# Gated linear attention with a routed mixture of experts on one core: where an exponential, a sigmoid and the first rows of a slot table stand in their queues, and which PSUM banks take transposed x

## The chip, the cores and the metric

The kernel runs on one core of a Trainium2 chip, in float32 apart from the half-precision tables described below. Its time is the device time of one execution in microseconds (us); several executions are timed and their median is given. A profile is one further execution, recorded by the hardware profiler, with every instruction's start and duration. Engines are called PE (TensorE, matrix products), DVE (VectorE), ACT (ScalarE), POOL (GpSimd) and SP (SyncE, which issues most DMA transfers). Each engine runs its own instructions strictly in the order of its queue, and waits on semaphores for the others.

## The reference

The input x has 8 sequences of 512 tokens with 512 features. With `xn = layernorm(x)` the output is `x + s * silu(f)`:

- `s` is linear attention with decay on xn: q, k, v and a gate are products of xn with weights; q and k pass a SiLU and a rotation; 16 heads of 32 features work in chunks of 128 tokens with a running state; the result is multiplied by a sigmoid gate, normalised by head, and projected by Wo.
- `f` is a mixture of 16 experts (each a SwiGLU with 128 hidden features), of which each token uses its 4 best, weighted by a softmax over those 4, plus one shared expert weighted by a sigmoid.

```
logits = xn @ gate_w.T                      # 16 per token
top 4 of softmax(logits), renormalised      # = exp(l - max) / sum over the 4
f = sum_r w_r * expert_{e_r}(xn) + sigmoid(xn @ shared_gate) * shared(xn)
out = x + attention(xn) * silu(f)
```

## The kernel before

**Stages.** (1) `first` walks the 8 sequences in pieces: it normalises x (`norm`), transposes it on PE (`turn`), computes router logits and the 4 best experts (`route_1` to `route_3`), and the shared expert (`share_1`, `share_2`). Sequence 0's attention (`enter`, `sequence(0)`) is interleaved with those pieces. (2) `sort` turns the choices of all 4096 tokens into places in lists by expert, in blocks of 128 rows. (3) `table` inverts the places into a slot table: which token stands in which row of which block. It runs beside the attention of sequence 1. (4) The 136 and more blocks are gathered, passed through their experts, scaled and written. (5) The attention of sequences 2 to 7 runs while the expert rows are gathered back and added up.

**What sets the order.** The program is traced line by line; a planner then fixes the order of each engine's queue by when it thinks each instruction is ready, the earlier traced one first among those that are. Two helpers overrule it. `on_pe()` (L206) queues a PE instruction behind the PE instruction traced last under it, so the order of nearly all PE work is that of the source. `behind(engine)` (L214) queues what its block traces behind the instruction of that engine traced last before it. Neither adds a wait for a result; they fix who stands ahead of whom. Anything else floats.

**PSUM banks.** `bank(tag, name)` (L106) gives a bank of 128 x 512 floats: four with the tag a, one k, one m, two d. A bank is handed on when its last reader is done. In `turn` (L272) each of a sequence's four tiles takes a bank, PE writes four 128 x 128 transposes into it, and ACT copies it out (L286). Other users of these tags near it: `share_1` writes pg to m and pu to d (L345, L346), `share_2` writes its four tiles to d, a, m, a (L364), `key` products go to m and `query` products and `output` to d, `value` to m and d by turns, the four score products of a head group to all four a (L704).

**Sort's tail.** `sort` is a generator. Its steps are drawn one at a time by `also()` inside `sequence(0)`; what is left after its loop over r (L419 to L433) is traced by L1041, after `sequence(0)` has ended, so after the four projections of sequence 0 and their copies out (`spill`, L983, an ACT copy to `so`). That tail is: the exponential of the 4 logits per token (L435, ACT), the sum, reciprocal and product (L437 to L439, DVE), the sigmoid of the shared gate (L441, ACT) and its store (L442), seven POOL instructions that spread the weights over the 16 experts into `wt` (L446, L450), the store of `wt` beside the rows of xn in DRAM (L451), and the store of the places `posi` (L454).

**Change of rooms.** All tiles of stages 1 and 2 live in the pool `p1`. L1043 closes it, and the pool `exps` is opened in its place with one tile, `wexp`, for the weights of all 16 experts (L1047). It covers the room in which posi, oh, w4, sgs, wt, wr and the others stood. Its first users are the weight loads of eleven experts (L1050, on SP's queue), and in the room of the last experts the tables of `table`: two small casts on ACT (L496, L498) and an iota on POOL that writes the counts 0, 1, 2, ... (L499). Seven stores of zeros to `y_d` follow on SP (L1054), and behind them the load of transposed x of sequence 2 (L584).

**The slot table.** 128 lists of 32 tokens' places (`sp`) are treated 16 at a time by `make(i)`: for each half of the 16, a comparison of the counts with the place inside half a block (L516), for the first half a product with the token number (L519), and a comparison with the number of the half block (L522), all on DVE. `number` multiplies the other half by its token numbers on ACT (L530, eight small instructions). PE then adds 16 products up in `pn` (L553), and DVE adds that to `acc` (L562, L564). `table` is a generator too: after its set-up, one step is drawn after each quarter of a key, query or value product of `sequence(1)` by `between[0]()` (L605, L649). So the first call of `make` (i = 0) is traced in the key product of group 2, behind the scores of group 0; the second (i = 16) in the query product of group 2. The first `pn` products stand under `on_pe()` between the third and fourth quarters of that query product. The last result gives `slot` (L573), by which the block rows are gathered.

**The PE order around it** is: projections of sequence 0 (pw, L800), states and scores of sequence 1's group 0 (L699, L710), key product of group 2 (L646), transposes of group 1's keys (L678, which reuse the bank of the states that DVE reads in L723 and L725), three quarters of the query product of group 2, the first pn (L553), and on.

Of the kernel before, what the change touches and what calls it, by code (L numbers as in the profile page):

```python
# [15 lines left out]
AF = mybir.ActivationFunctionType  # L16
ALU = mybir.AluOpType
# [28 lines left out]
HALF = P // 2  # L46
GROUP = 16
# [49 lines left out]
def tile_block(ctx: ExitStack, tc: tile.TileContext, a: dict, out: bass.AP):  # L97
    nc = tc.nc
# [7 lines left out]
    def bank(tag, name):  # L106
        return pp.tile([P, 512], F32, tag=tag, name=name, bufs={"a": 4, "k": 1, "m": 1, "d": 2}[tag])
# [39 lines left out]
    def load_x(b):  # L147
        t = p1.tile([P, NC, D], F32, tag="x", name=f"x_{b}", bufs=3)
        rows = x[b].rearrange("(t p) d -> p t d", p=P)
        for ts in [slice(i, i + 1) for i in range(NC)] if b == 0 else [slice(0, NC)]:  # L150
            nc.sync.dma_start(t[:, ts, :], rows[:, ts, :])
        xs_of[b] = t
# [36 lines left out]
    w4 = p1.tile([P, NT, TOPK], F32, tag="w4", name="w4")  # L189
    sgs = p1.tile([P, NT], F32, tag="sgs", name="sgs")  # L190
    posi = p1.tile([P, TOPK, NT], I32, tag="posi", name="posi")

    sp = const.tile([P, 2, TOPK * NT], F16, tag="slot", name="sp")
# [11 lines left out]
    @contextmanager  # L205
    def on_pe():  # L206

        with tc.issue_after(last_pe[-1]) if last_pe else nullcontext():
            yield
        traced = nc.cur_bb.bb.instructions  # L210
        last_pe.append(next(
            i for i in reversed(traced) if i.engine == mybir.EngineType.PE))

    def behind(engine):  # L214

        last = next(
            (i for i in reversed(nc.cur_bb.bb.instructions) if i.engine == engine), None)
        return tc.issue_after(last) if last else nullcontext()

    POOL, DVE, ACT = (  # L220
        mybir.EngineType.Pool, mybir.EngineType.DVE, mybir.EngineType.Activation)
# [50 lines left out]
    def turn(b):  # L272

        xs = xs_of[b]
        if b:
            xT = p1.tile([P, KC, N], F32, tag="xT1", name=f"xT1_{b}", bufs=2)
        else:
            xT = xT_of[b] = att.tile([P, KC, N], F32, tag="xT", name=f"xT_{b}", bufs=1)
        xT1_of[b] = xT
        for t in range(NC):  # L280
            ps = bank("a", f"psT_{b}_{t}")
            with on_pe():
                for k in range(KC):
                    nc.tensor.transpose(
                        ps[:, k * P : (k + 1) * P], xs[:, t, k * P : (k + 1) * P], ident)
            nc.scalar.copy(  # L286
                xT[:, :, t * P : (t + 1) * P], ps.rearrange("p (k n) -> p k n", n=P))
        if b:
            xs_of.pop(b)
            if b + 3 < B:  # L290
                load_x(b + 3)
            nc.sync.dma_start(xT_d[b], xT.rearrange("p k n -> p (k n)"))
# [80 lines left out]
    def sort():  # L373
# [5 lines left out]
        for to, by, name in ((total, ones, "total"), (af, tri, "before")):  # L379
            ps = bank("a", f"p{name}")  # L380
# [38 lines left out]
        for r in range(TOPK):  # L419
# [12 lines left out]
                    sp.rearrange("p w (r t) -> p w r t", t=NT)[:, :, r], bl[:, :, r])  # L432
            yield  # L433

        nc.scalar.activation(w4, w4, AF.Exp)  # L435
        den = p1.tile([P, NT], F32, tag="den", name="den")
        nc.vector.tensor_reduce(den, w4, axis=AX.X, op=ALU.add)  # L437
        nc.vector.reciprocal(den, den)
        nc.vector.tensor_tensor(  # L439
            w4, w4, den.unsqueeze(2).to_broadcast([P, NT, TOPK]), ALU.mult)  # L440
        nc.scalar.activation(sgs, sgs, AF.Sigmoid)  # L441
        nc.sync.dma_start(sg_d, sgs)  # L442
        wt = p1.tile([P, NT, E], F32, tag="h1", name="wt", bufs=2)
        wr = p1.tile([P, NT, E], F32, tag="sl", name="wr", bufs=2)
# [25 lines left out]
    def table(room):  # L470

        half = room.bitcast(F16)
        free = [0]
        quads = GROUP // QUAD


        def part(*shape):
            n = int(np.prod(shape))  # L480
            free[0] += n
            flat = half[:, free[0] - n : free[0]]
            return flat.rearrange("p (q j) -> p q j", j=QUAD) if len(shape) == 2 else (
                flat.rearrange("p (u q j) -> p u q j", u=quads, j=QUAD))

        homes = [(part(quads, HALF, QUAD), part(quads, 2 * NB, QUAD))]
        count = part(2 * NB, QUAD)
        free[0] = 2 * WE * (LATE - LATE // 2)
        homes.append((part(quads, HALF, QUAD), part(quads, 2 * NB, QUAD)))

        def flat(n):
            free[0] += n
            return half[:, free[0] - n : free[0]]

        half_token, fold, acc = flat(NT), flat(HALF), flat(2 * NB)
        nc.scalar.copy(half_token, token)  # L496
        for h in range(0, P, HALF):
            nc.scalar.copy(fold[h : h + HALF], ident[h : h + HALF, h : h + HALF])  # L498
        nc.gpsimd.iota(  # L499
            count, [[1, 2 * NB], [0, QUAD]], base=0, channel_multiplier=0,  # L500
            allow_small_or_imprecise_dtypes=True)

        def rows(of, n):
            return of.rearrange("p (u j) -> p u j", j=QUAD).unsqueeze(2).to_broadcast(
                [P, of.shape[-1] // QUAD, n, QUAD])

        def make(i):
            place, block = homes[i // GROUP % 2]
            for u in range(0, quads, quads // 2):
                us = slice(u, u + quads // 2)  # L510
                lists = slice(i + u * QUAD, i + (u + quads // 2) * QUAD)

                def counts(n):
                    return count[:, :n].unsqueeze(1).to_broadcast([P, quads // 2, n, QUAD])

                nc.vector.tensor_tensor(  # L516
                    place[:, us], counts(HALF), rows(sp[:, 0, lists], HALF), ALU.is_equal)
                if u == 0:
                    nc.vector.tensor_tensor(  # L519
                        place[:, us], place[:, us], rows(half_token[:, lists.start % NT :][  # L520
                            :, : GROUP // 2], HALF), ALU.mult)
                nc.vector.tensor_tensor(  # L522
                    block[:, us], counts(2 * NB), rows(sp[:, 1, lists], 2 * NB), ALU.is_equal)

        def number(i, some):
            place = homes[i // GROUP % 2][0]
            for j in range(max(some[0], GROUP // 2), some[1]):
                row = place[:, j // QUAD, :, j % QUAD]
                t = (i + j) % NT
                nc.scalar.activation(row, row, AF.Copy, scale=token[:, t : t + 1])  # L530

        yield
        make(0)
        for j in range(0, GROUP, 4):
            number(0, (j, j + 4))
            yield
        for i in range(0, TOPK * NT, GROUP):
            more = i + GROUP < TOPK * NT
            if more:
                make(i + GROUP)  # L540
            else:
                for e in range(E - LATE, E - LATE // 2):
                    nc.sync.dma_start(wexp[:, e, :], a["experts"][:, e, :])
            if i < TOPK * NT // 2:
                yield
            place, block = homes[i // GROUP % 2]
            pn = bank("a", f"pn_{i}")
            for some in ((0, 5), (5, 10), (10, GROUP)):
                if some[0] == 5:
                    with on_pe():  # L550
                        for j in range(GROUP):
                            h = j % 2 * HALF
                            nc.tensor.matmul(  # L553
                                pn[h : h + HALF, : 2 * NB],
                                lhsT=place[:, j // QUAD, :, j % QUAD],
                                rhs=block[:, j // QUAD, :, j % QUAD], start=(j < 2),
                                stop=(j >= GROUP - 2))
                if more:
                    number(i + GROUP, some)
                if some[1] == GROUP:  # L560
                    if i:
                        nc.vector.tensor_tensor(acc, acc, pn[:, : 2 * NB], ALU.add)  # L562
                    else:
                        nc.vector.tensor_copy(acc, pn[:, : 2 * NB])  # L564
                yield
        pt = bank("a", "pslot")
        with on_pe():
            for h in range(2):
                nc.tensor.matmul(
                    pt[h * HALF : (h + 1) * HALF, :NB], lhsT=fold,  # L570
                    rhs=acc.rearrange("p (b h) -> p b h", h=2)[:, :, h], start=True, stop=True)
        t = const.tile([P, NB], I32, tag="slot", name="slot")
        nc.vector.tensor_scalar(t, pt[:, :NB], float(B * N // 2), None, ALU.add)  # L573
        slots.append(t)
# [411 lines left out]
    def first():  # L986
# [22 lines left out]
        next(sorting)  # L1009

    sorting = sort()
    norm(0)
    turn(0)
    norm(1)
    halves(0)
# [196 lines left out]
    place = comb.tile([P, TOPK, NT], I32, tag="place", name="place")  # L1212
# [166 lines left out]
```

## Time and profile before

| what | us |
|---|---|
| median of 3 timed executions (1164.88 to 1168.21) | 1166.71 |
| the profiled execution's own time | 1162.74 |
| its span, from the first to the last instruction | 1160.9 |
| PE busy | 1128.0 |
| DVE busy | 710.2 |
| ACT busy | 456.3 |
| POOL busy | 454.1 |
| idle time of PE ahead of the transposes of the last sequence (at 155.9) | 1.05 |
| idle time of PE ahead of a value product (at 185.8) | 1.04 |
| idle time of PE ahead of the key transposes of sequence 1, group 1 (at 237.7) | 4.54 |
| idle time of PE ahead of a value product of sequence 2 (at 266.3) | 1.85 |
| first pn products start | 243.67 |
| first gather of block rows starts | 301.95 |

Times such as "at 243.67" count from the start of the span. In the answers of the trace a line of the timeline gives the start, the time taken, the engine, the line of the kernel, the operation, output and input, their shape and how many were merged, and in brackets how long the engine had stood idle and what ended that. A line with the name of an engine and a q (SPq) is that engine's queue issuing a transfer.

### The profile page before, as it was taken

What the parts mean: (1) busy time and instruction counts of PE and PEld (TensorE: products, weight loads), DVE (VectorE), ACT (ScalarE), POOL (GpSimd) and SP (SyncE); (2) the same over time, 40 slices, a digit from 0 to 9 for tenths busy, and PEclk for the clock granted to TensorE, in tenths of its full rate; (3) what the DMA queues carried; (4) which work ended last, traced back from release to release, by engine and by line L of the source; (5) the groups of instructions that cost most, each with busy time, mean ns of one, the idle gap of its engine ahead of it and who ended that gap; (6) DMA issues with size and microseconds to landing.
All of it is one profiled execution on the core that took longest, in us unless ns stands there. A gap on an engine that the chain in (4) does not pass through costs nothing. (4 is left out here: it accounts for less than half of the span.)

```text
span 1160.9 us, 21688 instructions
## 1 busy us (share of the span) xinstructions
PE 1128.0 (97%) x7782; PEld 686.9 (59%) x7782; DVE 710.2 (61%) x1496; ACT 456.3 (39%) x1044; POOL 454.1 (39%) x432
## 2 busy tenths in 40 slices
PE   7999999989999999999999999999999999999997
PEld 4445554445577777777777775555554645546453
DVE  6358735899134444444444444968879597697784
ACT  3224424154364444444444442363251532523541
POOL 3213103300223333333333331773877858858211
PEclk9999999989999999999999999999999999999999
DMA  9975431281869999999989896942746637544012
GB/s 330 325 271 202 160 112 46 78 324 54 249 164 229 230 229 223 236 228 229 221 226 227 228 223 188 355 119 81 267 126 195 201 110 254 151 122 146 25 38 73
DMA packets 163787, 217.45 MB, mean 187 GB/s; under 512 B 89824, under 2 KB 99168, under 8 KB 161760
## 3 DMA queue, kind: packets, MB, share of 16 engines
q1 hardware_dynamic: 142272, 144.14, 41.1%
q0 software_dynamic: 21120, 70.34, 21.9%
q8 instruction: 65, 1.06, 0.4%
q10 hardware_dynamic: 288, 1.57, 0.4%
q14 instruction: 42, 0.34, 0.1%
HBM read 125.73 MB, written 72.43 MB: 171 GB/s over the span
## 5 line engine op out<-in xcount | busy, mean ns | idle before, releaser
L1127 PE MATMUL pgu<-wexp,xt 128*128 x1088 | 257.4, 380 | 1.1 <-ACT xt L1108 0.6
L1127 PEld LDWEIGHTS pgu<-wexp,xt 128*128 128x128 f32 x1088 | 206.2, 190 | 87.7 <-issue 31.2
L1086 POOL DMA_INDIRECT xg<-xn_d,slot x79 | 74.8, 947 | 233.9 <-DVE y L1157 153.9
L1132 DVE TENSOR_TENSOR slb<-slb,pgu 128x128 f32<-128x128 f32 x136 | 39.1, 287 | 190.2 <-ACT slb L1131 190.2
L1110 ACT COPY xt<-pl 128x512 uint16<-128x512 uint16 x136 | 104.3, 767 | 130.0 <-DMA pl<-xg 72.6
L1230 POOL DMA_INDIRECT yg<-y_d,place x128 | 142.7, 1115 | 31.0 <-issue 18.3
L1148 PE MATMUL py<-wexp,hT 128*128 x272 | 139.2, 594 | 0.0
L602 PE MATMUL pv<-wv,xT 128*128 128x512 f32 x256 | 119.9, 609 | 2.9 <-DMA xT<-xT_d 1.9
L646 PE MATMUL pq<-xT,wq 128*128 128x512 f32 x256 | 118.3, 604 | 0.3 <-PEq L1192 0.3
L646 PE MATMUL pk<-xT,wk 128*128 128x512 f32 x256 | 118.2, 603 | 0.0
L800 PE MATMUL pw<-wo,on 128*128 128x512 f32 x224 | 100.6, 596 | 5.1 <-DVE m L1268 5.1
L1086 POOL DMA_INDIRECT more<-xn_d,slot x57 | 53.8, 944 | 108.1 <-DVE y L1157 107.2
L1272 POOL TENSOR_TENSOR xo<-xo,m 128x512 f32<-128x512 f32 x31 | 45.3, 1461 | 128.9 <-DVE m L1268 121.7
L646 PEld LDWEIGHTS pq<-xT,wq 128*128 128x128 f32 x256 | 48.1, 194 | 55.3 <-issue 53.9
L735 DVE TENSOR_TENSOR sc<-ps,dmask 128x512 f32<-128x512 f32 x128 | 79.0, 677 | 1.3 <-PE ps L710 1.2
L602 PEld LDWEIGHTS pv<-wv,xT 128*128 128x128 f32 x256 | 46.2, 191 | 53.4 <-issue 46.9
L1157 DVE TENSOR_SCALAR y<-py,xg 128x512 f32<-128x512 f32 x79 | 59.2, 750 | 29.3 <-PE py L1148 29.1
L646 PEld LDWEIGHTS pk<-xT,wk 128*128 128x128 f32 x256 | 46.2, 189 | 50.7 <-issue 48.3
L800 PEld LDWEIGHTS pw<-wo,on 128*128 128x128 f32 x224 | 41.2, 190 | 54.4 <-issue 45.4
L1131 ACT ACTIVATE slb<-pgu 128x128 f32<-128x128 f32 x136 | 37.9, 278 | 89.0 <-PE pgu L1127 88.6
L719 ACT COPY blocked<-state 32x96 f32<-32x96 f32 x96 | 30.8, 320 | 79.3 <-DVE state L714 78.5
L1157 DVE TENSOR_SCALAR y<-py,more 128x512 f32<-128x512 f32 x57 | 42.7, 750 | 20.7 <-PE py L1148 20.7
(176 smaller groups left out, 1712.3 us busy)
## 6 DMA issues: line engine op xcount, KB each, us to landing
y_d<-y SPq DMA_DIRECT2D x136, 256.0 KB, 3.1
wexp<-in_experts SPq DMA_DIRECT2D x14, 768.0 KB, 5.9
sh_d<-sh SPq DMA_DIRECT2D x32, 256.0 KB, 3.1
m<-sh_d SPq DMA_DIRECT2D x32, 256.0 KB, 4.0
xo<-in_x SPq DMA_DIRECT2D x32, 256.0 KB, 3.4
out<-xo SPq DMA_DIRECT2D x31, 256.0 KB, 2.1
x<-in_x SPq DMA_DIRECT2D x7, 1024.0 KB, 7.3
xT_d<-xT SPq DMA_DIRECT2D x7, 1024.0 KB, 3.9
```

The source lines that it names most:

```text
L602: nc.tensor.matmul(pv, lhsT=xT_of[b][:, k, t * P : (t + 1) * P], rhs=wv[:, k, :], start=(k == 0), stop=(k == KC - 1))
L646: nc.tensor.matmul(ps, lhsT=w[:, k, g * P : (g + 1) * P], rhs=xT_of[b][:, k, :], start=(k == 0), stop=(k == KC - 1))
L735: nc.vector.tensor_tensor(s, pss[j].rearrange("p (c t) -> p c t", t=C), dmask[:, g * HG + j].unsqueeze(1).to_broadcast([P, NC, C]), ALU.mult)
L800: nc.tensor.matmul(pw, lhsT=on_of[b][:, g, t * P : (t + 1) * P], rhs=wo[:, g, :], start=(g == 0), stop=(g == G - 1))
L1086: nc.gpsimd.indirect_dma_start(out=row(i), out_offset=None, in_=xn_d, in_offset=bass.IndirectOffsetOnAxis(ap=slot[:, i : i + 1], axis=0))
L1110: nc.scalar.copy(xt[:, KP:, :].bitcast(U16).rearrange("p k (t h) -> p h k t", h=2), turned(i).rearrange("p (h k) t -> p h k t", h=2))
L1127: nc.tensor.matmul(pg[:, : 2 * F], lhsT=xt[:, k, :], rhs=wflat[:, bass.ds(off + k * 2 * F, 2 * F)], start=(k == 0), stop=(k == KC - 1))
L1132: nc.vector.tensor_tensor(sl, sl, pg[:, F : 2 * F], ALU.mult)
L1148: nc.tensor.matmul(py, lhsT=hT_of.pop(i), rhs=wflat[:, bass.ds(off_of.pop(i) + KC * 2 * F, D)], start=True, stop=True)
L1157: gone.append(nc.vector.tensor_scalar(y, py, row(i).bitcast(F32)[:, bass.ds(at, 1)], None, ALU.mult).ins)
L1230: nc.gpsimd.indirect_dma_start(out=yg, out_offset=None, in_=y_d, in_offset=bass.IndirectOffsetOnAxis(ap=place[:, r, g : g + 1], axis=0))
L1272: nc.gpsimd.tensor_tensor(xo, xo, m, ALU.add)
```

## The change

There are three edits. In `turn`, the four tiles of every sequence but the first take the banks d, m, a, a in place of four a. In `sort`'s tail, the exponential and the sigmoid are each queued behind the ACT instruction traced last before them. In `make`, for i = 0 and i = 16 the comparison of L516 is queued behind the DVE instruction traced last before it; the product of L519 and the comparison of L522 are left as they were. No instruction is added or removed, and no value changes.

```diff
@@ turn
         for t in range(NC):
-            ps = bank("a", f"psT_{b}_{t}")
+            ps = bank("dmaa"[t] if b else "a", f"psT_{b}_{t}")
             with on_pe():
@@ sort
-        nc.scalar.activation(w4, w4, AF.Exp)
+        with behind(ACT):
+            nc.scalar.activation(w4, w4, AF.Exp)
         den = p1.tile([P, NT], F32, tag="den", name="den")
         nc.vector.tensor_reduce(den, w4, axis=AX.X, op=ALU.add)
         nc.vector.reciprocal(den, den)
         nc.vector.tensor_tensor(
             w4, w4, den.unsqueeze(2).to_broadcast([P, NT, TOPK]), ALU.mult)
-        nc.scalar.activation(sgs, sgs, AF.Sigmoid)
+        with behind(ACT):
+            nc.scalar.activation(sgs, sgs, AF.Sigmoid)
         nc.sync.dma_start(sg_d, sgs)
@@ table, make
-                nc.vector.tensor_tensor(
-                    place[:, us], counts(HALF), rows(sp[:, 0, lists], HALF), ALU.is_equal)
+                with behind(DVE) if i < 2 * GROUP else nullcontext():
+                    nc.vector.tensor_tensor(
+                        place[:, us], counts(HALF), rows(sp[:, 0, lists], HALF), ALU.is_equal)
                 if u == 0:
```

## The prediction, on record before the changed kernel ran

> **What bounds the kernel now.** I read the page's busy table first, then PE's timeline from 0 to 330 us for its idle brackets, then the timelines of ACT, POOL and SP around each, and the granted clock in 1 us windows.
>
> ```profile
> PE   1128.0 (97%) x7782; PEld 686.9 (59%) x7782; DVE 710.2 (61%) x1496; ACT 456.3 (39%) x1044; POOL 454.1 (39%) x432
> ...
> ```
>
> PE is the bound, and its order is pinned, so a change is worth what it does to PE's idle time and clock. The places that this change can reach:
>
> ```profile
> 155.86 2.42 PE L284 MATMUL psT<-ident,x 128*128 128x128 f32 x16 [1.05 <-DVE sc L735]
> 185.76 3.70 PE L602 MATMUL pv<-wv,xT 128*128 128x512 f32 x8 [1.04 <-ACT sh L369]
> 237.72 0.90 PE L678 MATMUL pk<-ident,kT 128*128 128x128 f32 x3 [4.54 <-DVE state L725]
> 243.67 1.23 PE L553 MATMUL pn<-wexp 128*64 128x286 f16 x16
> 266.26 4.29 PE L602 MATMUL pv<-wv,xT 128*128 128x512 f32 x6 [1.85 <-DMA xT<-xT_d]
> ```
>
> The first is turn's wait for four a banks still held by scores. The second is bank m, read late because ACT ran sigmoid and exponential first. The third is DVE doing the first two calls of make before the states. The fourth line has no idle time: pn's operands were ready at 234.3. The row that decides the case is another one, where the room of p1 becomes wexp:
>
> ```profile
> 188.99 1.38 POOL L446 TENSOR_TENSOR wt<-oh,w 128x512 f32<-128x512 f32 x1 [48.82 <-DVE w L439]
> ...
> 198.24 1.29 POOL L450 TENSOR_TENSOR wt<-wt,wr 128x512 f32<-128x512 f32 x1
> ...
> 226.59 3.24 POOL L499 IOTA wexp<- 128x572 f16 x1 [11.57 <-DMA at_d<-posi]
> ```
> ```profile
> 199.55 0.37 SPq L451 DMA_DIRECT2D xn_d<-wt  x1
> ...
> 224.72 0.32 SPq L454 DMA_DIRECT2D at_d<-posi  x1
> ...
> 226.40 0.81 SPq L1050 DMA_DIRECT2D wexp<-in_experts  x2
> ```
> ```profile
> 226.51 0.22 ACT L496 CAST wexp<-token 128x32 f16<-128x32 f32 x1 [4.59 <-DMA at_d<-posi]
> ```
>
> Weight loads (SP), a cast (ACT) and the iota (POOL) start within 0.2 us of each other, just after the store of posi landed (224.72 + 1.5 = 226.2). None of them reads posi, and they write different parts of wexp. So they wait for the whole room to be given up: wexp is one tile, and its first use waits for the last use of every p1 tile under it. The store of posi was last; wt's had landed at 204.
>
> **The change, part by part.** Times are of the profiled execution.
>
> *Banks.* For the last sequence the scores end at 154.8. Two tiles now go at once to d and m; the other two need the first two score banks, read by 155.8 and 156.4 (155.12, one each 0.62). PE is through at about 157.0, where the next product began at 158.12: gain 1.1. For sequence 4 the m bank has just been filled by a key product; its SiLU runs from 87.22 to 87.82 and the second tile, due at 87.5, starts at 87.9: loss 0.4. In three turns (43.9, 107.5, 132.8) the next product wants m right as ACT copies it out: 0.1 each, loss 0.3. Elsewhere the d and m banks were read well before. The planner may place other ACT and DVE work differently; bounds for all of this -1 to +1.2.
>
> *Exponential and sigmoid.* Leaving 183.7 to 187.8, they free ACT for the copy that PE awaited: gain 1.04. So the projections, whose last ended at 228.05, end 1.4 earlier (1.1 - 0.4 - 0.3 + 1.04): 226.65. But "the ACT instruction traced last" is by then the copy out of the fourth projection (L983), since L1041 traces this tail after the whole sequence. So the chain starts 41 us later than it did:
> - copy: 0.25 after its product, as at 217.85, and 0.59 long: 227.5.
> - table load 1.28 and exponential 0.31 (rows at 186.21 and 187.50): 229.1.
> - sum, reciprocal, product on DVE: 187.85 to 188.85, 1.0. DVE is on the scores now; one in progress costs 0.6, all four 2.5, the rotation behind them some 2.9 more. Being traced earlier than these, I take 0.6: 230.7.
> - seven POOL instructions, 188.99 to 199.53: 10.5, with 0.15 ahead: 241.4. (Their cover was 37 us of slack; it is gone.)
> - store of wt: 4.5 from issue to landing: 245.9. Behind it on SP stand all weight loads.
> - first users: 0.4 after landing, as for posi: 246.3, against 226.6.
> - iota to the last of the eight L530: 226.59 to 234.29, 7.7, and 0.2 to PE: pn can start at 254.2.
>
> PE comes to pn far sooner. The states are read at once, since DVE has nothing of make to do, so the 4.54 goes with its slow clock; key product, transposes and three quarters of the query product (3.6, 0.3, 2.6, from 228.1) bring PE to pn at about 234.7. There it stands some 19 us: the new wait takes the place of the old. Pinned behind pn are the rest of that query product and all later PE work. pn starts at 254.2, not 243.67: **+10.5**.
>
> *Clock.* In the 1 us windows the granted clock went to 0.50 after the 4.54 us wait and came back at about 243.6, 5.9 us after PE resumed; after the 1.85 us wait it was low from 267.5 to 270.9, 3.4 us. Half speed for 5.9 us costs 2.95, for 3.4 us 1.7. Before, full speed was back just as pn began; now the loss comes behind pn: **+2.3**.
>
> ```profile
> 242.00:243.00 1.00, 1.00 (x3) 0.17 (x1) 0.60 (x1) 0.00 (x0) 0.00 (x0) 0.50 1.02 416
> 243.00:244.00 1.00, 1.00 (x7) 0.30 (x8) 0.00 (x0) 0.00 (x0) 0.00 (x0) 0.69 1.06 430
> ```
>
> The Trainium skill, "TensorE: Matmul & The Clock Gate", section "What's actually happening", has half clock after an idle window of about 3.4 us and full clock after as long busy; the 1.85 us wait shows that less idle time can do here. By that page the clock's term would be an estimated 1.7.
>
> *Weight loads.* They and the zero stores move 19.9 later, from 246.3. Before, the traffic ended at about 258.5; a hole of some 1.6 us at 234 to 237, where SP waited for the last copy of a projection, closes: 276.8. The load of transposed x follows the query product that ended at 261.3, now 274.1. Behind the backlog it needs its 1 MB (2.7 at 390 GB/s) and some 0.8: 280.3, against 266.25 + 12.8 = 279.0: **+1.0**, bounds 0 to 3.
>
> *First rows of the slot table.* With the iota at 249.5, states and scores are past in any case; the hold on L516 finds its predecessors done. DVE stands idle, so make costs what it did: 0. Were it not so, the bounds are a loss of the 2.5 of the four scores and a gain of nothing. The gather of rows, all else and the end follow PE.
>
> Sum: 10.5 + 2.3 + 1.0 = +13.8. The profiled execution was 1162.74 with a span of 1160.9, so 1176.5 and 1174.7. It is 4 below the median of the runs, 1166.71; on that median I forecast **1180.5**.
>
> The Trainium skill, "ScalarE: Activation LUTs", section "What ACT_TABLE_LOAD costs", adds a drain of about 1.38 us to each load. In the trace a copy ended at 186.2, the load began at 186.21 and the exponential at 187.50, so no such drain shows. By the page the chain would be an estimated 1.4 longer, 1181.9.
>
> **Rivals.**
>
> *Faster: the room does not wait for wt.* If wexp's first users wait for posi's store alone, the iota runs 225.2 to 228.4, states and scores are first (to 230.8), make's part and L530 end at 235.3, and pn starts at 235.5, 8.2 earlier. The load of x then lies behind the weights (traffic to 255.5, landed at 259.0), 7.2 earlier than 266.25: 1159.5. Then the hold on L516 does its work. It decides if the weight loads start while POOL is still on wt. For it: only posi is named as the releaser. Against it: three engines released together by a store that none of them reads. 6%.
>
> *Much slower.* The three DVE instructions stand behind all scores and the rotation (4.8 more than I took), POOL loses time against DVE, and the load of x lies 3 late: 13.8 + 4.8 + 2 = +20.6, 1187. For it: DVE's queue is the planner's, and one wt row took 2.06 where the others took 1.3. 18%.
>
> *No change.* Were the hold's end the shared expert's last copy, exponential and wt would stay at 187 to 200 and only some 1.4 and the hold on L516 would count, which the unheld L522 (1.34 each, four of them) could eat. The source speaks against it: the copy of L983 is traced between. 3%.
>
> **How the numbers follow.** Forecast 73%, its own bounds 1175 to 1186 (no wait for DVE -0.6, wt at 1.3 each -1.4, clock 1.7 to 2.9, load of x 0 to 3, banks 1 either way); much slower 18%; faster 6%; no change 3%. Faster or slower counts from 0.3%, 3.5 us, about what a measurement of this kernel can tell from no change. The range leaves out the faster and the unchanged case (9%) and the far end of the much slower one: 1173 to 1190. Chances: faster 0.06, same 0.03, slower 0.91.
>
> **What would show it.** Right: exponential behind the fourth so copy near 229; wt on POOL from about 231 to 241; weight loads, cast and iota together near 246; PE idle some 19 us ahead of the first pn, released by L516 or L530, with clock 0.50 behind; the 1.04 ahead of pv and the 4.54 ahead of L678 gone; psT of the last sequence with an idle time in its midst and not ahead; x of sequence 2 landed near 280. Wrong: weight loads that start near 225, or an exponential that still stands near 187.

## The result, and the profile after

The changed kernel takes 1176.38 us (median; 1174.0 to 1183.5 in 4 runs), the kernel before 1166.74 beside it: ratio 1.0107, 95% interval 1.0079 to 1.0135. The medians lie 9.6 us apart; the ratio on record is not their quotient and would come to 12.5 us. By both the kernel is slower. The forecast was 1180.5 within 1173 to 1190. The profiled execution took 1183.5 with a span of 1181.7 and is the slowest of its four, so its places up to 311 us are used below and its end is not.

The line numbers move by one to three: L553 is now L556, L446 is L448, L451 is L453, L499 is L501, L1050 is L1053, L735 is L738. The busy row first:

```profile
PE 1132.3 (96%) x7782; PEld 690.7 (58%) x7782; DVE 715.2 (61%) x1496; ACT 456.9 (39%) x1045; POOL 454.9 (38%) x432
```

PE's work grew by 4.3 us, the span by 20.8: the rest is idle time. PE's list of waits (line, what released it, us in total, times, longest) puts one at the head that did not exist before:

```profile
PE pn L556 <- DVE wexp L522: 16.2, 1, 16.2
...
PE pn L556 <- DVE sc L738: 2.3, 2, 1.5
PE pv L605 <- DMA xT<-xT_d: 2.0, 1, 2.0
```

The 4.5 for the states (key transposes), the 1.05 for scores ahead of psT and the 1.04 for ACT's `sh` are off the list. In PE's timeline the places that answer to those of before:

```profile
154.78 2.37 PE L284 MATMUL psT<-ident,x 128*128 128x128 f32 x16
...
183.43 3.68 PE L605 MATMUL pv<-wv,xT 128*128 128x512 f32 x8
...
230.66 0.49 PE L681 MATMUL pk<-ident,kT 128*128 128x128 f32 x3
230.99 2.74 PE L649 MATMUL pq<-xT,wq 128*128 128x512 f32 x6
249.91 1.16 PE L556 MATMUL pn<-wexp 128*64 128x286 f16 x8 [16.18 <-DVE wexp L522]
251.51 1.26 PE L556 MATMUL pn<-wexp 128*64 128x286 f16 x8 [0.43 <-DVE wexp L525]
252.70 2.08 PE L649 MATMUL pq<-xT,wq 128*128 128x512 f32 x2
254.71 3.37 PE L635 MATMUL p<-g,wg 32*128 32x128 f32 x32
```

The first four rows have no bracket: the waits that the edits aim at are gone. The fifth has all of them and more in one. The last two rows take 2.08 and 3.37, where the same shapes took 1.13 and 1.80 before: half clock. What PE stood for is read from ACT, POOL, DVE and SP, in this order:

```profile
225.85 0.58 ACT L986 COPY so<-pw 128x512 f32<-128x512 f32 x1 [2.89 <-PE pw L803]
226.45 1.28 ACT L436 ACT_TABLE_LOAD   x1
227.74 0.31 ACT L436 ACTIVATE w<-w 128x128 f32<-128x128 f32 x1
...
244.51 0.22 ACT L498 CAST wexp<-token 128x32 f16<-128x32 f32 x1 [10.80 <-DMA xn_d<-wt]
```
```profile
229.17 1.82 POOL L448 TENSOR_TENSOR wt<-oh,w 128x512 f32<-128x512 f32 x1 [4.93 <-DVE w L440]
...
238.65 1.26 POOL L452 TENSOR_TENSOR wt<-wt,wr 128x512 f32<-128x512 f32 x1
244.57 3.24 POOL L501 IOTA wexp<- 128x572 f16 x1 [4.66 <-DMA xn_d<-wt]
```
```profile
247.84 0.42 DVE L519 TENSOR_TENSOR wexp<-wexp,sp 128x512 f16<-128x512 f16 x1 [10.49 <-POOL wexp L501]
```
```profile
221.09 0.32 SPq L456 DMA_DIRECT2D at_d<-posi  x1
...
239.94 0.37 SPq L453 DMA_DIRECT2D xn_d<-wt  x1
244.50 8.38 SPq L1053 DMA_DIRECT2D wexp<-in_experts  x11
```

The exponential's table load starts 0.02 after the fourth projection's copy ends (226.43), and the exponential follows it; POOL spreads the weights from 229.17 to 239.91; the store of `wt` is issued at 239.94, and at 244.5 the weight loads, the cast and the iota start together. The brackets of the cast and of the iota now name the store of `wt`, where before they named that of `posi`, although `posi` was stored at 221.09, earlier than before. The weight loads alone could have been kept by SP's queue, in which they stand behind that store; the cast and the iota are on other queues. So in both kernels the last user of the room sets its handing on, whichever that is.

### The profile page after: what moved, and what is told of

The parts are those of the page before. It is cut to its first block, busy times and chain, and to the rows that moved or that the text cites. A ratio compares the mean times of both kernels' runs of the same rounds, so it can differ in the third digit from the quotient of the medians.

```text
span 1181.7 us, 21687 instructions
## 1 busy us (share of the span) xinstructions
PE 1132.3 (96%) x7782; PEld 690.7 (58%) x7782; DVE 715.2 (61%) x1496; ACT 456.9 (39%) x1045; POOL 454.9 (38%) x432
## 5 line engine op out<-in xcount | busy, mean ns | idle before, releaser
L649 PE MATMUL pk<-xT,wk 128*128 128x512 f32 x256 | 118.4, 604 | 0.0
L649 PE MATMUL pq<-xT,wq 128*128 128x512 f32 x256 | 116.7, 597 | 0.3 <-PEq L1195 0.3
L738 DVE TENSOR_TENSOR sc<-ps,dmask 128x512 f32<-128x512 f32 x128 | 79.2, 676 | 0.7 <-PE ps L713 0.6
L649 PEld LDWEIGHTS pq<-xT,wq 128*128 128x128 f32 x256 | 47.4, 191 | 54.2 <-issue 53.0
L649 PEld LDWEIGHTS pk<-xT,wk 128*128 128x128 f32 x256 | 46.2, 189 | 50.9 <-issue 48.3
```

What stands on the lines that cost most here:

```text
L649: nc.tensor.matmul(ps, lhsT=w[:, k, g * P : (g + 1) * P], rhs=xT_of[b][:, k, :], start=(k == 0), stop=(k == KC - 1))
L738: nc.vector.tensor_tensor(s, pss[j].rearrange("p (c t) -> p c t", t=C), dmask[:, g * HG + j].unsqueeze(1).to_broadcast([P, NC, C]), ALU.mult)
```

## The experiments

Two theories at first. **Room**: nearly all of the loss is the exponential's new place, by the chain exponential, `wt`, store, room, iota, make. **Bank and DVE**: the new banks or the held comparison cost what was seen. Each ratio is against runs of the kernel before that were shared by the runs of one call (before's median: 1175.6 for e1 to e4, 1175.4 for e5 to e8, 1164.4 for e9 and e10). The ratios and intervals are those on record, and not always the quotient of the two medians (e7's medians give 1.0021). The slot table's last product, from which the gathers follow, serves as the mark of the early stage: 299.10 in before's first trace, 311.03 in the changed kernel's.

**e1: the held exponential and sigmoid alone.**

```diff
-        nc.scalar.activation(w4, w4, AF.Exp)
+        with behind(ACT):
+            nc.scalar.activation(w4, w4, AF.Exp)
...
+        with behind(ACT):
+            nc.scalar.activation(sgs, sgs, AF.Sigmoid)
```

> Only the exponential and the sigmoid are held behind the last ACT copy; banks and slot table as before. Theory (the room of p1 is given up late, because the store of wt comes late): nearly all of the loss is here, ratio to the kernel before 1.008 to 1.013; weight loads, cast and iota start together near 245, and PE stands 15 to 19 us ahead of the first pn. Rival (the loss comes from the three edits together, the hold on L516 above all): ratio below 1.004 and first pn before 246.

Measured: 1188.66, ratio 1.0100 (1.0056 to 1.0144), as much as the whole change. PE's timeline of e1:

```profile
251.13 1.16 PE L555 MATMUL pn<-wexp 128*64 128x286 f16 x8 [16.19 <-DVE wexp L521]
...
312.25 0.25 PE L571 MATMUL pslot<-wexp 128*64 128x143 f16 x2 [0.76 <-DVE on L795]
```

The wait of 16.2 is here without the other two edits, and the 1.04 ahead of pv is gone. So neither the hold on L516 nor the new banks make PE stand at pn.

**e2: the four banks alone.**

```diff
-            ps = bank("a", f"psT_{b}_{t}")
+            ps = bank("dmaa"[t] if b else "a", f"psT_{b}_{t}")
```

> Only the banks of the transposes change. Theory: the wait of 1.05 us ahead of the last sequence's transposes goes, 0.3 to 0.4 comes back at sequence 4, ratio 0.998 to 1.001, too little to be told from no change by time; the trace is to show it. Rival (d and m are wanted elsewhere and stall PE): ratio above 1.002.

Measured: 1173.7, ratio 0.9972 (0.9947 to 0.9998); slot table at 297.86. PE's timeline of e2:

```profile
88.21 1.53 PE L284 MATMUL psT<-ident,x 128*128 128x128 f32 x12 [0.25 <-ACT sk L656]
...
155.79 2.37 PE L284 MATMUL psT<-ident,x 128*128 128x128 f32 x16
```

The last sequence's transposes stand no more, and sequence 4's wait in their midst for bank m, which a key product has just filled. From the query product at 72 to the value product at 185.6 the two come to a gain of 0.46 (113.22 against 113.68). The ratio's interval only just leaves out 1, and the rest of it is not explained by these rows.

**e3: the held comparison alone.**

```diff
-                nc.vector.tensor_tensor(
-                    place[:, us], counts(HALF), rows(sp[:, 0, lists], HALF), ALU.is_equal)
+                with behind(DVE) if i < 2 * GROUP else nullcontext():
+                    nc.vector.tensor_tensor(
+                        place[:, us], counts(HALF), rows(sp[:, 0, lists], HALF), ALU.is_equal)
```

> Only the comparison of L516 is held for the first two calls of make. Theory: the comparison of L522 is not held and stays ahead of the states, four of 1.34 us and with them two of the second halves' L516, some 5.7 us where 7.1 stood, so the wait of 4.54 us ahead of the key transposes shrinks to about 3.2 and the ratio is 0.997 to 1.000. Rival (the hold does its work): the wait is gone, its slow clock with it, ratio 0.992 to 0.995. Second rival (a delayed make delays the first pn): ratio above 1.002.

Measured: 1175.42, ratio 1.0009 (0.9979 to 1.0039). PE's timeline of e3:

```profile
236.69 0.90 PE L679 MATMUL pk<-ident,kT 128*128 128x128 f32 x3 [3.20 <-DVE state L726]
...
245.24 1.15 PE L633 MATMUL p<-g,wg 32*128 32x128 f32 x22 [0.91 <-DVE wexp L565]
...
280.77 1.92 PE L554 MATMUL pn<-wexp 128*64 128x286 f16 x16 [1.98 <-DVE sc L736]
...
299.00 0.25 PE L570 MATMUL pslot<-wexp 128*64 128x143 f16 x2 [0.76 <-DVE on L794]
```

The wait for the states falls from 4.54 to 3.20, the comparison of L522 that floats still standing ahead of them. Two later waits for DVE give the gain back: the slot table comes at 299.00 against 299.10. That the work which DVE puts off at 232 is what PE waits for at 245 and 280 fits these rows, but was not tested by itself.

**e4: the changed kernel again, beside its parts.**

> The changed kernel once more, for a second profile beside the others. Theory: the first pn near 250 again, PE idle 16 us ahead of it, and up to the gathers 12 us late as in the first profile; the further 9 us by which the first profile was late at its end do not come back, so the ratio is 1.007 to 1.011. Rival (the change also slows the block stage): the block stage is again 5 us longer than before.

Measured: 1187.39, ratio 1.0101 (1.0068 to 1.0133); pn at 250.58 after 16.18, slot table at 309.62. The loss is the same in a call in which the kernel before takes 1175.6, and e1 has all of it. The second question of this run, whether the change also slows the block stage, stays open: from the slot table to the first query product of sequence 2 it is 419.5 in before, 424.8 in the changed kernel's first trace and 422.9 here, but also 420.2 in e1, 420.4 in e9 and 424.3 in e6.

**e5: the change, with one POOL instruction in place of seven.** The weights of the second to fourth choice are left out of `wt`.

```diff
-        for r in range(TOPK):
+        for r in range(1):
             nc.gpsimd.tensor_tensor(
-                wr if r else wt, oh[:, r].rearrange("p e t -> p t e"),
+                wt, oh[:, r].rearrange("p e t -> p t e"),
                 w4[:, :, r : r + 1].to_broadcast([P, NT, E]), ALU.mult)
-            if r:
-                nc.gpsimd.tensor_tensor(wt, wt, wr, ALU.add)
```

> The changed kernel with one POOL instruction in place of the seven that spread the weights (the weights of the second to fourth choice are left out). Theory: the chain from the late exponential to the room is what PE stands for, so each us taken out of it comes back: 10.7 us of POOL become about 1.8, the weight loads start some 9 us sooner, near 235.5, the wait ahead of the first pn falls from 16.2 to about 7.3, and the ratio falls from the changed kernel's 1.010 to 1.001 to 1.004. Rival (PE stands for make on DVE or for the weight transfers, which wt only happens to precede): the wait stays above 13.

Measured: 1180.48, ratio 1.0045 (1.0013 to 1.0078). SP's and PE's timelines of e5:

```profile
232.35 0.37 SPq L450 DMA_DIRECT2D xn_d<-wt  x1
...
236.99 9.23 SPq L1050 DMA_DIRECT2D wexp<-in_experts  x11
```
```profile
242.60 1.17 PE L553 MATMUL pn<-wexp 128*64 128x286 f16 x8 [7.55 <-DVE wexp L519]
...
305.91 0.26 PE L569 MATMUL pslot<-wexp 128*64 128x143 f16 x2 [0.76 <-DVE on L793]
```

From POOL's first instruction to the store of `wt` it is 1.9 in place of 10.8; the exponential stands 1.3 later in this execution, so the weight loads start 7.5 earlier than in the changed kernel, and PE's wait is 8.6 shorter. No weight load reads `wt`; POOL's time reaches them through the store and the room alone. The slot table comes only 5.1 earlier than in the changed kernel. The clock stayed at half till 257.1, 14.5 us after PE resumed; PE waited another 1.04 for DVE at 250.5; and half clock came again behind the load of x, where the value product at 273.06 took 4.47 and the changed kernel's 2.84.

**e6: the exponential and sigmoid behind the square root of sequence 0 (an ACT instruction at 196), the other parts as in before.**

```diff
+    mark = []
...
-        nc.scalar.activation(w4, w4, AF.Exp)
+        with tc.issue_after(mark[-1]):
+            nc.scalar.activation(w4, w4, AF.Exp)
...
-        nc.scalar.activation(rs, pr[:, :C], AF.Sqrt, bias=eps_rms, scale=1.0)
+        mark.append(nc.scalar.activation(rs, pr[:, :C], AF.Sqrt, bias=eps_rms, scale=1.0).ins)
```

> Kernel before, with exponential and sigmoid held behind ACT's square root of sequence 0's norm (L775), so only some 12 us later than before in place of 40. Theory: lateness as such costs nothing; the room opens with the later of the stores of posi and of wt, and wt's lands near 217, ahead of posi's 226. The 1.04 us ahead of the value product go; POOL's spreading now meets the products for the places (205 to 215), which may push posi's store back by up to 10 us. Ratio 0.998 to 1.006, weight loads from 225 to 235. Rival (the lateness of the exponential, or its table loads in the busier part of ACT's queue, is what costs): ratio above 1.008.

Measured: 1180.11, ratio 1.0031 (1.0006 to 1.0055), pn at 245.80. The store of `wt` is issued at 211.17, before that of `posi` (228.50), and the 16 us are gone. Yet something was lost. DVE's timeline of e6 shows where:

```profile
202.99 1.78 DVE L663 TENSOR_TENSOR kT<-sk,cos 128x512 f32<-128x512 f32 x1
204.69 1.85 DVE L664 TENSOR_TENSOR swk<-swk,sin 128x512 f32<-128x512 f32 x1
```

These took 0.67 and 0.68 in before. POOL's spread now runs from 199.8 to 211.1, beside the rotation; PE waits 2.49 for DVE ahead of the gate product, and the store of `posi`, which follows DVE, goes out at 228.5 in place of 224.7.

**e7: early exponential, banks for the last sequence alone, both comparisons of the first two calls of make held.** The exponential and the sigmoid stand behind the shared expert's last copy (L369).

```diff
-            ps = bank("a", f"psT_{b}_{t}")
+            ps = bank("dmaa"[t] if b == B - 1 else "a", f"psT_{b}_{t}")
...
-            nc.scalar.copy(sh, py)
+            mark.append(nc.scalar.copy(sh, py).ins)
...
+                with behind(DVE) if i < 2 * GROUP else nullcontext():
+                    nc.vector.tensor_tensor(
+                        block[:, us], counts(2 * NB), rows(sp[:, 1, lists], 2 * NB), ALU.is_equal)
```

> Kernel before with: exponential and sigmoid held behind the last copy of the shared expert only; d, m, a, a for the last sequence alone; and both comparisons of make (L516 and L522) held for i = 0 and 16. Theory: exponential near 186, room open at 224 to 225 as posi's store allows, states and scores ahead of all of make; the waits of 1.05, 1.04 and 4.54 us go and with the last its slow clock (2.9); first pn near 236 to 238; the load of x of sequence 2 then lies behind the weight loads, and 4 to 7 us are left: ratio 0.993 to 0.998. Rival (what is gained ahead of pn is given back to DVE, which is busy 93% of the time from 232 to 290): ratio 0.998 to 1.002, with pn waiting for scores.

Measured: 1177.86, ratio 1.0004 (0.9981 to 1.0027). PE's timeline of e7:

```profile
233.64 1.68 PE L558 MATMUL pn<-wexp 128*64 128x286 f16 x16
...
243.64 3.54 PE L715 MATMUL ps<-qT,kT 32*128 32x128 f32 x32 [2.77 <-ACT on L641]
247.11 5.04 PE L651 MATMUL pk<-xT,wk 128*128 128x512 f32 x6
...
296.13 0.26 PE L574 MATMUL pslot<-wexp 128*64 128x143 f16 x2 [0.76 <-DVE on L798]
```

PE reaches pn 10.0 earlier than in before and does not stand there. It stands 2.77 us ten microseconds later: make's second call came late on DVE, ACT's eight instructions for it (239.64 to 241.68) stood ahead of the sigmoid that frees a bank, and the clock fell to half from 244.9 to 251.3. Of ten microseconds three are left at the slot table, and none against before's second trace (e9, below).

**e8: e7, and the stores of zeros queued behind the load of x of sequence 2.**

```diff
+    def zeros():
+        none = att.tile([P, D], F32, tag="tmp", name="none", bufs=TMP)
+        nc.gpsimd.memset(none, 0.0)
+        with tc.issue_after(loads[-1]):
+            for i in range(SURE, NB):
+                nc.sync.dma_start(y_d[i * P : (i + 1) * P, :], none)
```

> As the three holds, and the seven stores of zeros queued behind the load of x of sequence 2 on SP, so that 1.8 MB less stand ahead of it. Theory: if the load of x is what takes gain back, PE's wait for it is 2 to 4 us shorter than with the three holds alone and the ratio 0.002 to 0.003 lower. Rival (DVE takes the gain back): no difference above 0.001.

Measured: 1177.47, ratio 1.0018 (0.9991 to 1.0045); slot table at 295.09. The wait for that load is 3.37, where e7 has 1.80: longer, not shorter. It is issued at 257.45, when the query product that frees its room is done, and PE is ready 3.1 us later. From its issue to PE's start it is 6.4 here and 4.9 in e7. In e7 the traffic ahead of it was over by 255 (DMA share 0.00 from 255 to 260); here the zeros are issued from 257.88 and run beside it. So there was nothing ahead of the load to take away, and the edit put traffic beside it.

**e9: the kernel before, unchanged, and e10: the two parts that gain.** In the traces of e1 to e8 PE waits some 3 us for "issue" at the states and scores of sequence 2 (from about 740 on; 2.4 to 4.2 in all up to 800), in all but e3 and e5 with the clock at half behind the first. Neither the trace of before nor that of the changed kernel has this. e10 has the early exponential and the banks of the last sequence as in e7, and make as in before.

> The kernel before, unchanged, so that its trace can be set beside those of the experiments. The slot table's last product (L569) starts at 299 by every theory. Theory 1, the waits of PE for issue (some 3 us at the first states of sequence 2 and later, with the clock at half behind them) that the experiments show and the first trace of before does not come with the device and not with an edit: they stand here too, and from the first query product of sequence 2 (718.6) to the end it takes 454 to 462 in place of 442.3. Theory 2, they come from the edited order: none here, and 442 to 445 from there to the end. The ratio to before is 1 within its interval, by either.

> Two edits alone: banks d, m, a, a for the transposes of the last sequence only, and exponential and sigmoid queued behind the shared expert's last copy; make is left as in before. Theory 1, both gains stay: the 1.05 ahead of psT and the 1.04 ahead of pv are gone, the fourth projection ends near 225.8 (before 228.05), the room opens 2.3 earlier, so do both the iota and make, and the 4.5 wait ahead of the key transposes stays: slot table's last product near 296.9, time 2.2 below before, ratio 0.998. Theory 2, what e7 and e8 lost after 300 (slot table 3 to 4 us earlier, time not lower) comes with the early exponential: slot table near 296.9 and ratio 1.001 to 1.004.

Measured: e9 1164.21, ratio 0.9990 (0.9967 to 1.0014); e10 1162.85, ratio 0.9991 (0.9967 to 1.0016). Neither trace has a wait for issue at 740. So an edited order can be without these waits, and e1 to e3, of which e2 and e3 hardly change it, all had them. The kernel before itself took 1175.6 and 1175.4 in the two calls whose traces have them, and 1164.4 in the call whose traces do not. This points to the device of the call and not to an edit; a trace of before in a call with these waits was not taken, so it is not shown. PE's timelines of e9 and then e10:

```profile
236.99 0.55 PE L678 MATMUL pk<-ident,kT 128*128 128x128 f32 x3 [4.54 <-DVE state L725]
...
296.07 0.26 PE L569 MATMUL pslot<-wexp 128*64 128x143 f16 x2 [0.76 <-DVE on L793]
```
```profile
235.40 0.90 PE L681 MATMUL pk<-ident,kT 128*128 128x128 f32 x3 [4.96 <-DVE state L728]
...
294.16 0.26 PE L572 MATMUL pslot<-wexp 128*64 128x143 f16 x2 [0.76 <-DVE on L796]
```

In e10 the slot table comes 1.9 earlier than in e9, about what the two gains come to (1.1 + 1.0). The ratio is in line with it, but its interval holds 1, so the time does not show a gain. e9's slot table also comes 3.0 earlier than in before's first trace with the same code: the mark itself moves by that much between executions, 0.7 of it ahead of 185 and 1.2 by the clock at 238 to 244.

Not tried: to keep `wt`, `oh` and `w4` outside the room that `wexp` takes, which would leave its handing on to the store of `posi`. Whether they would find room beside `wexp`, which takes 16 x 1536 floats of each partition, no run shows.

## Why the prediction was right, and where its sizes were off

**The mechanism** stands. The likeliest case happened at its place and in its order, e1 shows that the exponential's place alone makes the loss, and e5 that it runs through POOL and the room. The rival "the room does not wait for `wt`" falls with the first view of SP after the change; so does "the hold ends at the shared expert's copy", which e7 and e10 had to be built to get. Not all of its signs came: the first pn was released by the product with the token number (L519, now L522) and not by L516 or L530, PE stood 16.2 and not 19, and no idle time shows in the midst of the last sequence's transposes, though they took 2.37 where undisturbed ones take 1.91.

**Sizes.** By the slot table the loss was 11.9 in the profiled execution (311.03 - 299.10), against 13.8 forecast. Before's second trace (e9) has the mark at 296.07, so a single difference of this kind is uncertain by some 3 us. That the sum came so near is in part luck: pn came 4.3 earlier than forecast, and what lies behind pn lost 2.4 more.

| step | forecast | measured |
|---|---|---|
| transposes, from the query product at 72 to their end | +1.1 - 0.4 - 0.3 | gain 1.17, loss 0.71 |
| bank m read earlier, pv | gain 1.04 | gain 1.2 |
| copy of the fourth projection done | 227.5 | 226.43 |
| exponential done | 229.1 | 228.05 |
| DVE's three done | 230.7 | 229.08 |
| POOL's seven done | 241.4 | 239.91 |
| room open | 246.3 | 244.50 |
| first pn | 254.2 | 249.91 |
| first pn, against before | +10.5 | +6.2 |
| first pn to slot table, against before | +3.3 | +5.7 |

The first step that was off is the projections' end. The sum reckoned 1.4 earlier and it came 2.3 earlier; 0.67 of the rest stood already at the query product (71.41 against 72.08) and is not the edits' doing: before's first execution waited 0.92 for a weight transfer at 13.6, and the changed kernel's did not. Next, DVE was free and the 0.6 for a score in progress was not needed. The largest error is the step from the room to pn: the forecast had pn wait for the last of ACT's eight instructions (7.7 + 0.2 by before's rows). In fact pn's first eight products need only what DVE makes, and PE began them 5.4 after the room opened. The other eight began at 251.51, released by DVE, while ACT's eight still ran (250.23 to 252.27). That is 2.5 of the 4.3; the other 1.8 stood when the room opened.

The other way went the part behind pn. The **clock** was put at +2.3 with a bound of 2.9; the four rows behind pn (L649, L635, L754, L760) took 2.08 + 3.37 + 1.50 + 1.78 = 8.73 where before had 4.87, so it cost 3.9. The granted clock in windows of 1 us (the number ahead of the last two is the clock) of the changed kernel and then of e4, the same code:

```profile
253.00:254.00 1.00, 1.00 (x2) 0.20 (x1) 1.00 (x3) 0.00 (x0) 0.00 (x0) 0.50 1.07 434
260.00:261.00 1.00, 1.00 (x28) 0.92 (x24) 0.47 (x2) 0.71 (x2) 0.00 (x0) 0.54 1.03 424
261.00:262.00 1.00, 1.00 (x53) 0.96 (x49) 0.51 (x2) 0.00 (x0) 0.00 (x0) 1.00 1.04 424
```
```profile
254.00:255.00 1.00, 1.00 (x2) 0.00 (x0) 1.00 (x4) 0.00 (x0) 0.00 (x0) 0.50 0.97 399
255.00:256.00 1.00, 1.00 (x16) 0.64 (x18) 1.00 (x1) 0.53 (x2) 0.00 (x0) 0.85 1.01 399
```

Full speed is back 11.0 us after PE resumed in one and 4.7 in the other, after the same wait of 16.2. It took 5.9 in before and 3.9 in e9, after the same 4.54, and 14.5 in e5, after 7.55. PE was not dense in that time: it stood 0.43 between the halves of the first pn, and small products followed. What decides between 4.7 and 11.0 for the same code, no run shows. The Trainium skill, "TensorE: Matmul & The Clock Gate", section "What's actually happening", has full clock after about 3.4 us of sustained work, in a window that runs freely; e10 (2.8), e3 (3.4) and e9 (3.9) come near that, and the others here took up to four times as long.

The **load of transposed x** was put at +1.0 (the places it is worked out from, 280.3 and 279.0, give 1.3) and cost nothing: its wait is 1.96 against 1.85. Besides, the half clock that followed it in before (the value product took 4.29) does not follow it after (2.84), a gain of 1.5 that was not forecast. **Make** was put at 0: DVE stood idle from 237 to 247.8 and then had make, the rotation and the scores at once, so that two later pn products wait for scores 2.3 together, where before had 0.22. pn's own two halves add 1.6. With 0.45 off one score product, these terms come to 3.9 + 1.6 + 2.1 - 1.5 - 0.45 = 5.7, as measured. One reading of the prediction that no term uses was off too: it gives the weights' chain 37 us of slack, but by its own rows `wt` had landed at 204 and `posi` at 226.2, so the room left it 22.

**What stays open.** The held comparison's own worth cannot be told from nothing (e3, interval 0.9979 to 1.0039). e7 and e8 have their slot table 1.5 and 2.5 ahead of the mean of before's two traces (297.6), but their medians stand 2.5 and 2.1 above before's. For e7 a time 1.5 below before lies inside the interval; for e8 one 2.5 below (0.998) does not. The part from the first query product of sequence 2 to the end takes 461 to 462 in the profiles of e2, e6, e7 and e8 and 454 to 455 in those of e1, e3, e4 and e5, against 442 to 446 in those of before, the changed kernel, e9 and e10. These are single executions, and no run tells chance from order there.

## What to carry to other kernels

Before an instruction is held in a queue, follow what it feeds down to the handing on of memory: in this kernel the room was given up by the last user of any tile in it, so a chain whose data nobody needs before the first gather of rows (301.95) became the one that opens the room for everything that follows. "Behind the instruction traced last" is a place in the source and not a time: look up which instruction that is. And where an engine other than the bound holds the work, a hold moves its wait to the next place (e3, e7), so cost the second call too and not only the first.

## What was not expected of the hardware

**Small VectorE work beside GpSimd.** Operations on 16 elements per partition took six to seven times as long while POOL spread the weights. DVE's timeline of before, and then of the changed kernel, where POOL was idle:

```profile
195.64 1.06 DVE L392 TENSOR_SCALAR ci<-incl 128x16 int32<-128x16 f32 x1
196.73 0.18 DVE L394 TENSOR_SCALAR ci<-ci 128x16 int32<-128x16 int32 x1
196.94 1.25 DVE L397 CAST nb<-ci 128x16 f32<-128x16 int32 x1
```
```profile
192.62 0.18 DVE L392 TENSOR_SCALAR ci<-incl 128x16 int32<-128x16 f32 x1
192.83 0.17 DVE L394 TENSOR_SCALAR ci<-ci 128x16 int32<-128x16 int32 x1
193.04 0.17 DVE L397 CAST nb<-ci 128x16 f32<-128x16 int32 x1
```

The time lost does not follow the size: it is at most about one POOL instruction (1.3 to 2.1), and the next operation again takes 0.18. e6 shows the same on operations of 512 elements (0.68 to 1.85), there on the path. The Trainium skill, "SBUF — State Buffer", section "Who interferes with whom", describes a shared pair of ports that one of the two engines holds for a whole instruction; a loss of at most one POOL instruction agrees with that.

**Half clock without a long wait.** A wait of 1.85 us was followed by half clock in before (267.5 to 270.9), waits of 1.68 in e9 and 1.96 in the changed kernel at the same place by none. e2 (1.85) and e5 (1.92) have half clock there too, e6 (1.87) has not, so the length of the wait alone does not decide.

**Waits for issue.** In e1 to e8 the many short products of the states of sequence 2 stood up to 1.2 us at a time with "issue" as the reason, which means that the profile shows nothing that they waited for. PE's timeline of e8:

```profile
738.52 0.26 PE L706 MATMUL pk<-v,kd 128*32 128x32 f32 x3 [1.19 <-issue]
```

The clock was at 0.52 from 740 to 744 there, with the DMA share at 1.03. In before, with the DMA share at 1.04 in the same place, there was neither, so full DMA engines alone do not explain it.
